# GRU state summed in place in PSUM, multiplied there, and copied to SBUF afterwards

## Chip, cores and metric

The kernel runs on one core of a Trainium2 chip. The metric is the device time of one execution in microseconds. Before the change, three runs gave 2057.22, 2060.13 and 2060.7 us; the median is 2060.13.

## What is computed

A recommendation model for 1024 users (the leading dimension of the inputs), each with 100 historical items of 128 features. A GRU runs over the items, an attention MLP scores every state against the target item, a softmax over time weights the states, and a second recurrence (AuGRU) uses the weighted sum. The part that the change touches is this:

```
def gru_step(h, x_t):
    gi = x_t @ gru_Wih.T + gru_bih
    gh = h @ gru_Whh.T + gru_bhh
    i_r, i_z, i_n = jnp.split(gi, 3, axis=-1)
    h_r, h_z, h_n = jnp.split(gh, 3, axis=-1)
    r = jax.nn.sigmoid(i_r + h_r)
    z = jax.nn.sigmoid(i_z + h_z)
    n = jnp.tanh(i_n + r * h_n)
    h_new = (1.0 - z) * n + z * h
    return (h_new, h_new)
...
feat = jnp.concatenate([keys, q, keys - q, q * keys], axis=-1)
score = _mlp(feat, [(att_W0, att_b0), (att_W1, att_b1), (att_W2, att_b2)], jax.nn.relu)
```

`keys` are the GRU states of all steps and `q` is the target item, so the first attention layer needs two data-dependent inputs for each step: the state h and the product q * h.

## The kernel before

Everything is held transposed: 128 features on the partitions, users along the free dimension. The 1024 users are two halves of 512, each an object of class Half. [...] All instructions are issued in an order written out by hand, and each engine works through its own list in that order; waits between engines are put in for each dependence on a tile or a buffer.

The GRU phase loops over the steps s from 0 to 99. In a step each half runs `gru` (L497): TensorE makes the gates pr, ph, pi and pz, each in a PSUM tile named ps, of which six buffers are used in turn (L222). Each gate is cut into four column groups of 32 that run beside each other. ScalarE makes r from pr (L520). VectorE makes u from ph and r (L528), adds it to pi in place (L538), ScalarE takes tanh of pi in place (L539) and the sigmoid of pz in place (L540), and VectorE ends with h - n, times z, plus n (L543, L544, L545). The last of these writes the new state hn to SBUF, where TensorE reads it as an operand in the next step. Between them VectorE transposes the state of the step before for storage (L557).

After the gates of both halves, `attend(s-1)` (L661) issues the attention matmuls for the state of the step before: hn with wk, the product kq with wkq, and the deeper layers (mv with w12) of earlier steps, all into two PSUM tiles pm (one for each half, two buffers, L223). `take(s-2)` (L694), run in the next step right after r of half 0, adds q0 to pm (f, L704) and applies the relu (mv, L709), and sends a row of scores to s_b. Directly behind `take`, `product(s-1)` (L579) multiplies the state of each half by the item, SBUF with SBUF (kq, L583). Scores of a block of steps are turned into softmax weights in three stages on VectorE (L750 to L799), one stage at a time, after half 0's gates. The stage called scores uses one of the two pm buffers for a transposed tile pt, which L760 reads.

GpSimd multiplies the inputs by the mask and sums them (L493, L494), and sums the weighted states (kw, L606, and pooled, L607). Its share of the pooling at the very end is done beside VectorE. Then come indirect gathers and the AuGRU phase, which is untouched by the change.

The SP queue issues nearly all loads and stores, in program order. At the start it loads wih, x of step 0 for half 0, the biases, x of step 0 for half 1, whh; then, from step 0's gates, x of steps 1 and 2 for both halves; then, in `attention_weights` (L225), item (512 KB) and the attention weights.

Of the kernel before, what the change touches and what calls it, by code (L numbers as in the profile page):

```python
# [9 lines left out]
F32 = mybir.dt.float32  # L10
# [9 lines left out]
P = 128  # L20
B = 1024
T = 100
HB = 512
NH = B // HB
# [13 lines left out]
QA, QB = (2, 3), (3, 2)  # L38
# [40 lines left out]
def kernel(ctx: ExitStack, tc: tile.TileContext, a: dict, out: bass.AP):  # L79
# [26 lines left out]
    nc = tc.nc  # L106
# [22 lines left out]
    item = const.tile([P, B], F32, name="item")  # L129
# [56 lines left out]
    def gru_phase(pools):  # L186
# [7 lines left out]
        x_second = xp.tile([P, HB], F32, name="x")  # L194
        nc.sync.dma_start(out=x_second, in_=a["hist_x"][0][:, HB:])
        whh = load("whh", [P, 3, P])
        pre = pools.enter_context(tc.tile_pool(name="pre", bufs=1))

        brz = const.tile([P, 2], F32, name="brz")
# [15 lines left out]
            nc.gpsimd.memset(s_bs[j], 0.0)  # L215
        q0 = pre.tile([P, B], F32, name="q0")

        hp = pools.enter_context(tc.tile_pool(name="hp", bufs=6))
        wp = pools.enter_context(tc.tile_pool(name="wp", bufs=2))
        sp = pools.enter_context(tc.tile_pool(name="sp", bufs=2))  # L220
        kp = pools.enter_context(tc.tile_pool(name="kp", bufs=3 * NH))
# [1 line left out]
        pa = pools.enter_context(tc.tile_pool(name="pa", bufs=2, space=PSUM))  # L223

        def attention_weights():  # L225
            nc.sync.dma_start(out=item, in_=a["item"])
            w0 = load("w0", [P, 4, A0])
            for i in range(NH):
                for f, s in F0[i]:
                    nc.vector.tensor_add(wk[i][:, f], w0[:, 0, s], w0[:, 2, s])  # L230
                    nc.vector.tensor_copy(wkq[i][:, f], w0[:, 3, s])
                    nc.vector.tensor_sub(wq[i][:, f], w0[:, 1, s], w0[:, 2, s])
                    for f1, s1 in F1[i]:
                        nc.sync.dma_start(out=w12[i][f, f1], in_=a["w1"][s, s1])
                    nc.sync.dma_start(out=bm[i][f, :], in_=a["b0"][s, :])
                sc = slice(SC[i], SC[i] + 1)
                for f1, s1 in F1[i]:
                    nc.sync.dma_start(out=w12[i][f1, sc], in_=a["w2"][s1, :])
                    nc.sync.dma_start(out=bm[i][f1, :], in_=a["b1"][s1, :])
                nc.sync.dma_start(out=bm[i][sc, :], in_=a["b2"].partition_broadcast(1))  # L240
# [219 lines left out]
        class Half:  # L460
            def __init__(self, i):
                self.i = i
                self.cols = ts(i, HB)
                self.ks = ts(i, KH)
                self.h = {}
                self.mv = self.first = None
                self.todo = []
                self.x = {0: x_second if i else x_first}
                self.m = {}
                self.kt = {}  # L470
                self.s_bs = s_bs[i::NH]


            def load(self, t, again=False):
                if t or again:
                    x = xp.tile([P, HB], F32, name="x")
                    nc.sync.dma_start(out=x, in_=a["hist_x"][t][:, self.cols])
                    self.x[t] = x
# [16 lines left out]


            def gru(self, t, after_gate, after_sum):  # L497

                x = self.x[t]
                h = self.h[t - 1] if t else hist[:, self.cols]  # L500
                hn = hp.tile([P, HB], F32, tag="h", name="hn")
                self.h[t] = hn

                def gate(g, parts):
                    p = ps.tile([P, HB], F32, tag="g", name=f"ps{g}")
                    for j, (w, v) in enumerate(parts):
                        for q in range(P // R):
                            nc.tensor.matmul(  # L508
                                p[ts(q, R), :],
                                lhsT=w[:, g, ts(q, R)],  # L510
                                rhs=v,
                                start=(j == 0),
                                stop=(j == len(parts) - 1),
                            )
                    return p

                both = ((wih, x), (whh, h)) if t else ((wih, x),)
                pr = gate(0, both)
                r = wp.tile([P, HB], F32, tag="r", name="r")
                nc.scalar.activation(r, pr, AF.Sigmoid, bias=brz[:, 0:1])  # L520
                after_gate()
                if t:
                    ph = gate(2, ((whh, h),))
                pi = gate(2, ((wih, x),))
                pz = gate(1, both)
                u = wp.tile([P, HB], F32, tag="u", name="u")
                if t:
                    nc.vector.scalar_tensor_tensor(  # L528
                        out=u,
                        in0=ph,  # L530
                        scalar=bhh[:, 2:3],
                        in1=r,
                        op0=ALU.add,
                        op1=ALU.mult,
                    )
                else:
                    nc.vector.tensor_scalar_mul(u, r, bhh[:, 2:3])
                nc.vector.tensor_add(pi, pi, u)  # L538
                nc.scalar.activation(pi, pi, AF.Tanh, bias=bih[:, 2:3])  # L539
                nc.scalar.activation(pz, pz, AF.Sigmoid, bias=brz[:, 1:2])  # L540
                after_sum()
                d = wp.tile([P, HB], F32, tag="d", name="d")
                nc.vector.tensor_sub(d, h, pi)  # L543
                nc.vector.tensor_mul(d, pz, d)  # L544
                nc.vector.tensor_add(hn, pi, d)  # L545

            def transpose(self, t):

# [20 lines left out]
            def store(self, q):  # L569
# [4 lines left out]
                    ],  # L574
                    in_=self.kt[q].rearrange("p k n c -> p k (n c)"),
                )


            def product(self, t):  # L579

                h = self.h[t]
                kq = wp.tile([P, HB], F32, name="kq")
                nc.vector.tensor_mul(kq, h, item[:, self.cols])  # L583
                self.first = h, kq


            def pool(self, count, eng):
# [68 lines left out]
        halves = [Half(i) for i in range(NH)]  # L656
# [4 lines left out]
        def attend(t):  # L661

            p = left[t] = [pa.tile([P, HB], F32, tag="a", name="pm") for _ in halves]

            old = [half.mv if t else hist[:, half.cols] for half in halves]
            k_rows = slice(0 if t <= T else 2 * R, P)

            def pack(i, q, w, v, start, stop):
                s = ts(q, R)
                nc.tensor.matmul(p[i][s, :], lhsT=w[:, s], rhs=v, start=start, stop=stop)  # L670

            def first(i, q, j):
                if t < T:
                    w = (wk, wkq)[j][i]
                    pack(i, q, w, halves[i].first[j], j == 0 and q != QB[i], j == 1)

            def more(i, q):
                pack(i, q, w12[i][k_rows, :], old[i][k_rows, :], True, q == QA[i] or t >= T)

            for turn in range(2 * NH):  # L680
                i, j = divmod(turn, 2)
                for q in range(2):
                    first(i, q, j)
                if i == 0:
                    for q in range(2, P // R):
                        more((QA, QB)[j].index(q), q)
                else:
                    for q in range(2, P // R):
                        first(QB.index(q), q, j)
# [128 lines left out]
        def gather_early(n):  # L818
            for _ in range(n):
                next(more_early)  # L820
# [3 lines left out]
        for s in range(T):  # L824
            last = s == T - 1
            n, due = divmod(s - again, 4)
            n, i = divmod(n, NH)
            more_history = 0 <= n < late

            def loads():  # L830
                for half in halves:
                    for m in range(1, AHEAD + 1) if s == 0 else (AHEAD,):
                        if s + m < T:
                            half.load(s + m)
                            if s + m >= late:
                                half.load_mask(s + m)
                    if s == T - AHEAD:
                        half.load_features()
                if more_history and due == 0:
                    halves[i].load(n, again=True)  # L840
                    halves[i].load_mask(n)

            def after_gate():
                if s:
                    take(s - 2)
                    for half in halves:
                        half.product(s - 1)
                loads()

            staged = None  # L850
            for half in halves:
                half.gru(
                    s,
                    after_gate if half.i == 0 else nothing,
                    (lambda: half.transpose(s - 1)) if s else nothing,
                )
                if half.i == 0:
                    staged = bool(soft["stages"])
                    stage(0 if last else 1)
# [35 lines left out]
                next(features[f])  # L895

        gather_early(4)
        take(T - 2)
        for half in halves:
            half.product(T - 1)  # L900
        attend(T - 1)
        stage(2)
        weights = soft["e"][0]
# [45 lines left out]
        for half in reversed(halves):  # L949
            t = blocked(s_bs[NH * (soft["j"] % 2) + half.i])  # L950
# [402 lines left out]
```

## Time and profile before

| what | value |
|---|---|
| median of three runs | 2060.13 us |
| the profiled execution's own time | 2054.49 us |
| its span in the profile | 2052.7 us |
| PE busy | 1998.8 us (97%) |
| DVE busy | 1763.7 us (86%) |
| ACT busy | 824.5 us (40%) |
| POOL busy | 1313.0 us (64%) |
| GRU loop, end of its gates | about 1386 us from the span's start |

The page gives one execution. A group's row names line, engine and operation, output and inputs by the program's names, the shape and the count; then the busy time in microseconds and the mean of one in ns; then the idle time of the engine just before and what ended it. PE is TensorE, DVE is VectorE, ACT is ScalarE, POOL is GpSimd, SP is the queue that issues loads and stores. A row of the timeline gives the start in microseconds from the span's start, the time taken, the engine, line and operation, and in brackets the idle time ahead of it and its releaser. Busy shares are averages over two phases: in slices of the page PE is at 90% or more nearly everywhere but for the first slice and those between 1400 and 1480 us.

### The profile page before, as it was taken

The numbers are of one execution on the slowest core, as the hardware profiler recorded it, in microseconds if no ns is written. First come the engines' busy times: TensorE is split into PE (matmuls) and PEld (weight loads), VectorE is DVE, ScalarE is ACT, GpSimd is POOL, SyncE is SP. The second block draws the span as 40 slices with busy tenths as digits, with TensorE's granted clock in tenths as the row PEclk, the third lists the DMA queues.
The fourth block names the chain that finished last, engine by engine and source line by source line (L and its number), as shares of the span: only waits on it lengthen the run. The fifth ranks groups of instructions, "written<-read, shape, count | busy, mean of one in ns | idle before, by whom it ended". The sixth has DMA issues, their size and how long they took to land.

```text
span 2052.7 us, 41040 instructions
## 1 busy us (share of the span) xinstructions
PE 1998.8 (97%) x15452; PEld 1049.1 (51%) x15452; DVE 1763.7 (86%) x3066; ACT 824.5 (40%) x1508; POOL 1313.0 (64%) x1291
## 2 busy tenths in 40 slices
PE   8999999999999999999999999998699999999998
PEld 4655433333455544444443333334344556679997
DVE  6888999998999999989999899997377777888886
ACT  3334343333434343434343343343244444445554
POOL 0234939569797969695979787998543354443431
PEclk9999999999999999999999999999799999999999
DMA  4453233332334334333433232333432333333332
GB/s 121 97 115 105 89 105 113 96 93 78 104 113 114 108 109 124 113 99 110 135 105 100 85 99 77 102 105 103 117 101 88 94 110 98 94 102 85 93 72 37
DMA packets 241643, 205.65 MB, mean 100 GB/s; under 512 B 59270, under 2 KB 204394, under 8 KB 241434
## 3 DMA queue, kind: packets, MB, share of 16 engines
q1 hardware_dynamic: 227498, 170.43, 29.4%
q0 software_dynamic: 12352, 32.31, 5.7%
q8 instruction: 123, 2.02, 0.4%
q14 instruction: 86, 0.70, 0.1%
q10 hardware_dynamic: 1584, 0.20, 0.1%
HBM read 146.82 MB, written 54.40 MB: 98 GB/s over the span
## 4 chain that ended last, share of the span: by engine, by line
PE 83%; DVE 9%; issue 2%; DMA 2%; ACT 1%; POOL 1%; another core or an unknown queue 1%; SPq 0%; DVEq 0%; ACTq 0%; POOLq 0%
PE ps L508 42%; PE pm L670 14%; PE ph L1076 5%; PE pr L1076 4%; PE pu L1076 4%; PE pr L1072 4%; PE pu L1072 4%; PE ph L1072 4%; DVE kq L583 1%; DMA rows<-keys_d,idx_k 1%; DVE ps L538 1%; DVE d L544 1%; DVE d L543 1%; DVE u L528 1%; ACT ps L539 1%
## 5 line engine op out<-in xcount | busy, mean ns | idle before, releaser
L508 PE MATMUL ps<-x,wih 128*32 128x512 f32 x4800 | 778.3, 595 | 4.6 <-DMA x<-in_hist_x 4.0
L508 PE MATMUL ps<-hn,whh 128*32 128x512 f32 x4752 | 768.1, 592 | 0.0
L508 PEld LDWEIGHTS ps<-x,wih 128*32 128x32 f32 x4800 | 260.2, 110 | 291.0 <-issue 270.2
L508 PEld LDWEIGHTS ps<-hn,whh 128*32 128x32 f32 x4752 | 258.2, 110 | 280.1 <-issue 271.9
L539 ACT ACTIVATE ps<-ps,bih 128x512 f32<-128x512 f32 x200 | 132.4, 662 | 546.5 <-DVE ps L538 546.5
L493 POOL TENSOR_TENSOR xm<-x,m 128x512 f32<-128x512 f32 x200 | 248.1, 1240 | 121.7 <-DMA m<-mask_d 60.8
L494 POOL TENSOR_TENSOR hist<-hist,xm 128x512 f32<-128x512 f32 x200 | 269.7, 1349 | 15.7
L174 POOL DMA_INDIRECT rows<-keys_d,idx_k x220 | 213.9, 972 | 86.5 <-POOL rows L173 50.0
L607 POOL TENSOR_TENSOR pooled<-pooled,kw 128x512 f32<-128x512 f32 x191 | 257.6, 1349 | 15.0
L670 PE MATMUL pm<-hn,wk 128*32 128x512 f32 x1200 | 257.1, 592 | 4.0 <-DVE f L704 2.3
L606 POOL TENSOR_TENSOR kw<-kt,e 128x512 f32<-128x512 f32 x191 | 220.1, 1153 | 62.2 <-DVE e L779 62.1
L670 PE MATMUL pm<-kq,wkq 128*32 128x512 f32 x1200 | 257.2, 592 | 0.0
L520 ACT ACTIVATE r<-ps,brz 128x512 f32<-128x512 f32 x200 | 137.6, 688 | 285.6 <-PE ps L508 285.1
L670 PE MATMUL pm<-mv,w 128*32 128x512 f32 (+1 forms) x808 | 240.5, 592 | 8.2 <-DVE e L760 8.2
L583 DVE TENSOR_TENSOR kq<-hn,item 128x512 f32<-128x512 f32 x200 | 233.0, 1204 | 0.0
L1084 ACT ACTIVATE c<-ph,bh 128x96 f32<-128x96 f32 (+41 forms) x198 | 96.4, 487 | 292.6 <-PE ph L1076 248.3
L173 POOL COPY rows<-rest 128x1 f32<-128x1 f32 x188 | 35.3, 188 | 215.4 <-DVE rest L1113 211.7
L543 DVE TENSOR_TENSOR d<-hn,ps 128x512 f32<-128x512 f32 x198 | 136.1, 687 | 34.9 <-ACT ps L539 32.4
L1100 DVE TENSOR_TENSOR pu<-pu,c 128x96 f32<-128x96 f32 (+41 forms) x197 | 88.2, 448 | 86.0 <-ACT c L1084 77.4
L538 DVE TENSOR_TENSOR ps<-ps,u 128x512 f32<-128x512 f32 x200 | 140.0, 700 | 23.7 <-PE ps L508 3.1
L544 DVE TENSOR_TENSOR d<-ps,d 128x512 f32<-128x512 f32 x200 | 138.3, 691 | 22.7 <-ACT ps L540 3.4
L704 DVE TENSOR_TENSOR f<-pm,q 128x512 f32<-128x512 f32 x200 | 128.0, 681 | 26.5 <-PE pm L670 26.4
(180 smaller groups left out, 3101.5 us busy)
## 6 DMA issues: line engine op xcount, KB each, us to landing
x<-in_hist_x SPq DMA_DIRECT2D x212, 256.0 KB
keys_d<-kt SPq DMA_DIRECT2D x48, 1024.0 KB
m<-mask_d SPq DMA_DIRECT2D x200, 128.0 KB
rows<-keys_d,idx_k POOLq DMA_INDIRECT x220
s_b<-mv SPq DMA_DIRECT2D x200, 8.0 KB
keys_d<-kt SPq DMA_DIRECT2D x32, 64.0 KB
at<-att_d SPq DMA_DIRECT2D x34, 48.0 KB
mask_i<-in_mask SPq DMA_DIRECT2D x8, 200.0 KB
```

What stands on the lines that cost most here:

```text
L174: nc.gpsimd.indirect_dma_start(out=r[:, at, :], out_offset=None, in_=keys_d[q], in_offset=bass.IndirectOffsetOnAxis(ap=idx_k[:, k, i : i + ...
L493: nc.gpsimd.tensor_mul(d, x, m)
L494: nc.gpsimd.tensor_add(acc, acc, d)
L508: nc.tensor.matmul(p[ts(q, R), :], lhsT=w[:, g, ts(q, R)], rhs=v, start=(j == 0), stop=(j == len(parts) - 1),)
L538: nc.vector.tensor_add(pi, pi, u)
L544: nc.vector.tensor_mul(d, pz, d)
L583: nc.vector.tensor_mul(kq, h, item[:, self.cols])
L606: eng.tensor_mul(d, k, w)
L607: eng.tensor_add(acc, acc, d)
L670: nc.tensor.matmul(p[i][s, :], lhsT=w[:, s], rhs=v, start=start, stop=stop)
L1072: nc.tensor.matmul(p, lhsT=m[:, 1, :], rhs=k, start=True, stop=False)
L1076: nc.tensor.matmul(p, lhsT=m[:, 0, :], rhs=v, start=False, stop=True)
```

## The change

The last sum of the GRU step writes the new state over n in the PSUM tile pi, and the product with the item is taken at once from there, as the next VectorE instruction. The copy of the state to the SBUF tile hn becomes a ScalarE instruction of its own (`keep`): for half 0 it is issued after r of half 1 in the same step, for half 1 after r of half 0 in the next step, ahead of `take`, and after the last step ahead of the final `take`. The method `product` and its calls go. The item is loaded by SP right after whh, since the product of step 0 now needs it within that step. The pool of hn has five buffers in place of six, that of kq four in place of two.

```
         whh = load("whh", [P, 3, P])
+        nc.sync.dma_start(out=item, in_=a["item"])
...
-        hp = pools.enter_context(tc.tile_pool(name="hp", bufs=6))
+        hp = pools.enter_context(tc.tile_pool(name="hp", bufs=5))
...
         def attention_weights():
-            nc.sync.dma_start(out=item, in_=a["item"])
             w0 = load("w0", [P, 4, A0])
...
-                self.mv = self.first = None
+                self.mv = self.copy = None
+                self.first = {}
...
                 nc.vector.tensor_sub(d, h, pi)
                 nc.vector.tensor_mul(d, pz, d)
-                nc.vector.tensor_add(hn, pi, d)
+                nc.vector.tensor_add(pi, pi, d)
+                kq = wp.tile([P, HB], F32, name="kq", bufs=2 * NH)
+                nc.vector.tensor_mul(kq, pi, item[:, self.cols])
+                self.first[t] = hn, kq
+                self.copy = hn, pi
+
+            def keep(self):
+
+                if self.copy is not None:
+                    nc.scalar.copy(*self.copy)
+                    self.copy = None
...
-            def product(self, t):
-
-                h = self.h[t]
-                kq = wp.tile([P, HB], F32, name="kq")
-                nc.vector.tensor_mul(kq, h, item[:, self.cols])
-                self.first = h, kq
...
-                    pack(i, q, w, halves[i].first[j], j == 0 and q != QB[i], j == 1)
+                    pack(i, q, w, halves[i].first[t][j], j == 0 and q != QB[i], j == 1)
...
             def after_gate():
+                halves[1].keep()
                 if s:
                     take(s - 2)
-                    for half in halves:
-                        half.product(s - 1)
                 loads()
...
-                    after_gate if half.i == 0 else nothing,
+                    after_gate if half.i == 0 else halves[0].keep,
...
         gather_early(4)
+        halves[1].keep()
         take(T - 2)
-        for half in halves:
-            half.product(T - 1)
         attend(T - 1)
```

## The prediction

> **What bounds the kernel now.** I read the page first: engines, slices, groups; then who waited for whom on TensorE, then the timeline of one step and of the end of the GRU phase. From the page, first the chain, then the DVE groups that the change touches and two like the new product:
>
> ```profile
> PE 83%; DVE 9%; issue 2%; DMA 2%; ACT 1%; POOL 1%; another core or an unknown queue 1%; SPq 0%; DVEq 0%; ACTq 0%; POOLq 0%
> L583 DVE TENSOR_TENSOR kq<-hn,item 128x512 f32<-128x512 f32 x200 | 233.0, 1204 | 0.0
> L543 DVE TENSOR_TENSOR d<-hn,ps 128x512 f32<-128x512 f32 x198 | 136.1, 687 | 34.9 <-ACT ps L539 32.4
> L538 DVE TENSOR_TENSOR ps<-ps,u 128x512 f32<-128x512 f32 x200 | 140.0, 700 | 23.7 <-PE ps L508 3.1
> ```
>
> TensorE carries 83% of the chain. The product at L583 takes 1204 ns where equal-sized operations with an operand in PSUM take 690 to 700. TensorE's waits inside the GRU loop (60 to 1398 us) are few:
>
> ```profile
> engine line waited for: us in total, times, longest us
> PE pm L670 <- DVE e L760: 8.2, 7, 2.1
> PE pm L670 <- DVE f L704: 2.3, 1, 2.3
> PE ps L508 <- DVE u L528: 0.7, 2, 0.5
> PE count L323 <- issue: 0.3, 1, 0.3
> ```
>
> So 1338 us of loop hold 11.2 us in which TensorE waits for VectorE, and no GRU change can take more out of it, since no matmul is removed. Asked in stretches of 20 us, the view puts these waits at about 240 to 265, 380, 500, 1300, 1340 to 1375 (2.5 us) and 1393: where softmax or sorting work is added to a VectorE that is already full. One ordinary step, from the timeline:
>
> ```profile
> 711.67 0.69 DVE L545 TENSOR_TENSOR hn<-ps,d 128x512 f32<-128x512 f32 x1
> 712.28 1.28 DVE L704 TENSOR_TENSOR f<-pm,q 128x512 f32<-128x512 f32 x2
> 713.45 0.69 ACT L520 ACTIVATE r<-ps,brz 128x512 f32<-128x512 f32 x1 [2.75 <-PE ps L508]
> 713.48 2.99 DVE L583 TENSOR_TENSOR kq<-hn,item 128x512 f32<-128x512 f32 x2
> 715.88 1.52 POOL L606 TENSOR_TENSOR kw<-kt,e 128x512 f32<-128x512 f32 x1
> 716.39 0.74 DVE L528 SCALAR_TENSOR_TENSOR u<-ps,bhh,r 128x512 f32<-128x512 f32 x1
> ```
>
> A step lasts 13.73 us (the r at L520 of half 0 began at 699.71 and again at 713.45). VectorE needs some 13.1 of it: two chains from u to hn of 4.46 us each (703.37 to 707.83), two sums f 1.2, two products 2.9. It keeps 0.6 us, less than any softmax stage. GpSimd's kw beside the products takes 1.52 us, elsewhere 1.07.
>
> **The Trainium skill.** "SBUF — State Buffer", Who interferes with whom: a VectorE instruction with two SBUF inputs contends with a GpSimd instruction that reads SBUF; one with at most one does not. The trace agrees: the first two products, with GpSimd idle, took 1.28 us together, later pairs up to 2.99. "PSUM — Partial Sum Buffer", PSUM bank collisions raise a hardware error: two engines may not touch one bank at once, two reads included. In the changed program's order the ScalarE copy indeed waits for the product, not only for the sum; no run here shows a collision.
>
> **The change part by part.** *Product.* 200 products go from 1204 ns to about 690 (L543, the same operand kinds): 200 x 0.51 = 103 us of VectorE, about 1.0 a step on average and 1.5 in steps such as that shown (2.9 to 1.4). Nearly all lies beside TensorE. Its worth is the stalls it ends. The product also leaves its place ahead of half 0's u and stands behind each hn sum: half 0's chain starts some 2.9 us sooner, half 1's u stands 0.69 later behind it, but not later than before.
>
> *Sum into PSUM.* 700 ns (L538) for 691 (L545): 200 x 0.01 = 2 us of VectorE, hidden.
>
> *Copy.* 200 ScalarE copies PSUM to SBUF. The nearest row is the copy at L1027, 128x512 out of PSUM in 0.58 us: 116 us more for an engine busy 40%. The state is usable 0.69 + 0.58 + about 0.1 = 1.4 us later than now. Half 0: its sum ends at 707.9, first use in the next step at 712.25; 4.3 us of cover. Half 1: its copy is queued behind the next step's r of half 0, which ends at 714.14, so the copy ends at about 714.8. TensorE's half-1 gates begin 12 weight-load groups of 0.43 us after the step's first load at 710.96: loads at 716.1, matmuls at 716.5, and they also need that copy, because pr of half 1 takes the PSUM buffer of pi of half 1 (six buffers in turn, eight tiles a step). Cover 1.7 us; with it gone, each missing 0.1 us costs 10 us over 100 steps. Behind the copy on ScalarE stand the two mv (0.6 each) and tanh; mv is used at the end of the step, 7 us later, and tanh waits for VectorE anyway. The s_b transfers behind mv on SP start 0.6 us later, needed steps later.
>
> *Buffers.* hn from 6 to 5: a buffer is rewritten after its last reader, the attention pack one step on. kq from 2 to 4: the same. Cost nothing.
>
> *Item load moved* ahead of four x loads on SP's queue: 512 KB. The DMA rates of the first 8 us add up to some 1.5 MB, and item ends 1.44 MB into the order, so it lands before the first product at 11.5. The x of step 1 comes 1.6 us later, about 9, needed at 11.4. Nothing lost. But the first steps have no slack: copy of half 0 ends at 12.9 where the state was used at 12.24; the sum of half 1 then ends at 16.3 (15.5 now), its product at 17.0, its copy at 17.7, and half 1's pr waits for that where it began at 16.5. VectorE begins step 1 some 0.2 later, and the product of half 0 stands ahead of half 1's u in the chain to the q0 activations that free the attention banks (25.85 now). Together about +0.9 us; bounds 0 and 2.5.
>
> *Gain in the loop.* With 1.0 to 1.5 us freed per step, VectorE has about 2 us free, and the scores of a stage end about 0.9 us before TensorE's attention pack instead of after it. In the last steps a stage costs some 2.3 us a step and just fits. I take all 8.9 us of the waits before 1380.
>
> *Gain at the end.* Now:
>
> ```profile
> 1391.66 0.69 DVE L545 TENSOR_TENSOR hn<-ps,d 128x512 f32<-128x512 f32 x1
> 1393.46 2.30 DVE L583 TENSOR_TENSOR kq<-hn,item 128x512 f32<-128x512 f32 x2
> 1395.68 0.71 DVE L756 STREAM_TRANSPOSE last<-s_b 128x512 f32<-128x512 f32 x1
> 1400.41 1.08 POOL L596 TENSOR_TENSOR pooled<-pooled,e 128x512 f32<-128x512 f32 x1 [0.61 <-issue]
> 1401.68 1.07 POOL L606 TENSOR_TENSOR kw<-kt,e 128x512 f32<-128x512 f32 x1 [0.20 <-DVE e L779]
> ```
>
> The last gates end at 1386.3 and the second f at 1399.7, and VectorE is busy throughout. Without its lag the last sum ends 2.4 us after the gates (0.3 to the gate's end, 0.65 sigmoid, 0.7 times z, 0.7 sum) instead of 6.0. One product behind it makes 3.1, the two f that free the attention banks 4.4, and the attention pack on TensorE 3.4 more: the next f starts 7.8 us after the gates, since the softmax stage (2.8 us on VectorE) is done by 7.2. Now it starts at 1398.5, 12.2 after the gates: a gain of 4.4. VectorE and TensorE thus arrive 8.9 - 0.9 + 4.4 = 12.4 us earlier. GpSimd does not: from 1329.7 it runs to 1400 without a real wait. It reaches 1329.7 earlier by the waits until then, 8.9 - 2.5 - 0.9 = 5.5, plus 1.3 for a wait on e that goes; from there it gains three contended pairs of kw and pooled (0.45 + 0.33 each), 2.3, and 0.4 of small waits. That is 9.5, and the later one counts: **-9.5 us**. From there to the AuGRU loop the chain passes through GpSimd's sums, gathers and transfers of unchanged length, and that loop is unchanged.
>
> 2052.7 - 9.5 = 2043.2 of span. The profiled execution took 2054.49 us, so 2045.0; the median of the runs is 5.6 above it, and the prediction is 2060.1 - 9.5 = 2050.6.
>
> **Rivals.** (a) *GpSimd does not hold the end*: what it stores up earlier is larger. For it: kw waits for e 12 times in the loop, 61.9 us. Against: 18 to 19 of each 20 us busy after 1280. -12.4 and 1 to 2 us more from rows no longer disturbed after 1400: 2046. (b) *Gain hidden*: VectorE's stages stay late because their small SBUF operations still meet GpSimd (L784, 32 columns, 1298 ns), and the start costs its full 2.5: half of 8.9 and of 4.4 stays, 6.6 is gained less 2.5, and GpSimd passes on about 3: 2057. (c) *Slower*: half 1's copy comes too late for the PSUM buffer. Place: pr of half 1, each step. It decides once the copy ends over 1.7 us later than I put it; half a microsecond beyond costs 50 us: 2110. Against: product and sum end near 713.0, before r. (d) *The product is no faster from PSUM*: nothing to gain but the order, 2059. Against: three groups at 690 to 700 ns with that operand.
>
> **How the numbers follow.** Likeliest 0.57, (a) 0.13, (b) 0.17, (c) 0.08, (d) 0.05. About 0.2% (4 us) is what a measurement of this kernel can tell from no change. Faster: 0.57 + 0.13 + half of (b) = 0.79; same: half of (b) and most of (d) = 0.12; slower 0.09. The likeliest alone spans 2046 to 2055 (start 0 to 2.5, gain at the end 2.2 to 6); with (a) and most of (b) the range is 2044 to 2058.
>
> **What would show it.** Right: the product near 690 ns, copies near 0.58 us, TensorE's waits on e and f under 2 us in the loop, kw near 1.08 everywhere, q0 about 1 us later at the start, the step still 13.73 us. Wrong: TensorE waiting for ScalarE at L508 step after step; products above 1 us; waits on e still several microseconds; a gain in the loop that does not reach the AuGRU phase.

## The result

Six runs of the changed kernel have a median of 2049.09 us (2044.58 to 2050.1); six runs of the kernel before beside them have 2059.01 us (2055.69 to 2060.7). The ratio is 0.9949, with a 95% interval of 0.9936 to 0.9962: about 10 us faster. The profiled execution took 2046.78 us with a span of 2045.0 us (before 2054.49 and 2052.7).

Of the page after, first the chain of work that ended last, then the groups of the GRU step (busy us, mean ns of one, then the idle time ahead of them and what ended it):

```profile
PE 92%; DVE 3%; DMA 2%; issue 1%; ACT 1%; another core or an unknown queue 1%; POOL 0%; SPq 0%; DVEq 0%; ACTq 0%; POOLq 0%
```

```profile
L539 DVE TENSOR_TENSOR ps<-ps,u 128x512 f32<-128x512 f32 x200 | 140.0, 700 | 21.5 <-PE ps L509 0.5 <-DVE u L529 0.5
L548 DVE TENSOR_TENSOR kq<-ps,item 128x512 f32<-128x512 f32 x200 | 138.2, 691 | 6.9
L544 DVE TENSOR_TENSOR d<-hn,ps 128x512 f32<-128x512 f32 x198 | 136.1, 687 | 35.6 <-ACT ps L540 35.2 <-issue 0.2
```

```profile
L555 ACT COPY hn<-ps 128x512 f32<-128x512 f32 x200 | 116.6, 583 | 92.3 <-DVE kq L548 92.3
L609 POOL TENSOR_TENSOR kw<-kt,e 128x512 f32<-128x512 f32 x191 | 206.0, 1078 | 70.6 <-DVE e L782 70.6
```

The product takes 691 ns instead of 1204, like its neighbours with a PSUM operand, which have not moved. The copy costs 583 ns, and what it waits for is the product (kq), not the sum. GpSimd's kw is at 1078 ns. VectorE's part of the chain fell from 9% to 3%. TensorE's waits in the GRU loop and its end (60 to 1398 us), by whom it waited for:

```profile
engine line waited for: us in total, times, longest us
PE pm L673 <- ACT hn L555: 2.5, 1, 2.5
PE pm L673 <- ACT mv L712: 0.4, 1, 0.4
```

All waits for e and f are gone; the one of 2.5 us stands after the last gates. One ordinary step, from the timeline (start, duration, idle time ahead in brackets):

```profile
703.30 0.70 DVE L546 TENSOR_TENSOR ps<-ps,d 128x512 f32<-128x512 f32 x1
704.03 0.69 DVE L548 TENSOR_TENSOR kq<-ps,item 128x512 f32<-128x512 f32 x1
704.95 1.08 POOL L609 TENSOR_TENSOR kw<-kt,e 128x512 f32<-128x512 f32 x1
705.27 1.29 DVE L707 TENSOR_TENSOR f<-pm,q 128x512 f32<-128x512 f32 x2 [0.55 <-PE pm L673]
706.99 0.69 ACT L521 ACTIVATE r<-ps,brz 128x512 f32<-128x512 f32 x1 [4.49 <-PE ps L509]
707.57 0.58 ACT L555 COPY hn<-ps 128x512 f32<-128x512 f32 x1
707.91 0.75 DVE L529 SCALAR_TENSOR_TENSOR u<-ps,bhh,r 128x512 f32<-128x512 f32 x1 [1.36 <-PE ps L509]
```

VectorE now waits for TensorE in an ordinary step (0.55 ahead of f, 1.36 ahead of u); before, its longest gap in such a step was 0.18 us. The copy of half 1 ends at 708.15. TensorE's matmuls of x for half 1 begin at 710.03, and those of hn, which read the copy, at 710.88. The wait for the copy stands at the last of four weight loads ahead of them:

```profile
710.46 0.25 PEld L509 LDWEIGHTS ps<-hn,whh 128*32 128x32 f32 x4 [0.18 <-issue]
```

That one begins at 710.60 in the trace, 2.45 us after the copy's end. This distance is called the copy's cover below. The end of the GRU phase, VectorE and GpSimd, then TensorE's last attention pack:

```profile
1380.37 0.69 DVE L548 TENSOR_TENSOR kq<-ps,item 128x512 f32<-128x512 f32 x1
1380.98 1.28 DVE L707 TENSOR_TENSOR f<-pm,q 128x512 f32<-128x512 f32 x2
1388.44 1.29 DVE L707 TENSOR_TENSOR f<-pm,q 128x512 f32<-128x512 f32 x2 [3.32 <-PE last L640]
1391.16 1.07 POOL L609 TENSOR_TENSOR kw<-kt,e 128x512 f32<-128x512 f32 x1 [2.71 <-DVE e L782]
...
1381.80 1.05 PE L673 MATMUL pm<-hn,wk 128*32 128x512 f32 x4 [2.55 <-ACT hn L555]
1385.15 1.44 PE L673 MATMUL pm<-kq,wkq 128*32 128x512 f32 x5
```

The gates end at 1374.83 (the first attention matmul behind them), 11.4 us sooner than before (1386.27). GpSimd waits 2.71 us for e: it does not hold the end. The last f starts 1.85 us after the pack ends at 1386.59.

To say where the time went I cut each trace at three points: the ninth r (loop entry, step 4 of half 0), the end of the last gates, and the first AuGRU state. The last column is the last f, from the gates' end.

| | loop entry | loop, to the gates' end | gates' end to first AuGRU state | last f |
|---|---|---|---|---|
| before | 59.28 | 1326.99 | 54.67 | 12.3 |
| changed | 60.68 | 1314.15 | 55.59 | 13.6 |
| difference | +1.40 | -12.84 | +0.92 | +1.3 |

That is -10.5 us up to the AuGRU phase. In this pair of traces 2.8 us of it are lost later, in code that did not change; in these two and the four traces of the first chip below (chips differ, see the experiments), its length from the second state on varies between 590.0 and 597.1 us, so the medians (-9.9) are the better measure of the whole.

### The profile page after: what moved, and what is told of

Read it like the earlier page. It is cut to its first block, busy times and chain, and to the rows that moved or that the text cites. A ratio compares the mean times of both kernels' runs of the same rounds, so it can differ in the third digit from the quotient of the medians.

```text
span 2045.0 us, 41241 instructions
## 1 busy us (share of the span) xinstructions
PE 1994.6 (98%) x15452; PEld 1176.7 (58%) x15452; DVE 1682.1 (82%) x3066; ACT 944.1 (46%) x1708; POOL 1260.7 (62%) x1291
## 4 chain that ended last, share of the span: by engine, by line
PE 92%; DVE 3%; DMA 2%; issue 1%; ACT 1%; another core or an unknown queue 1%; POOL 0%; SPq 0%; DVEq 0%; ACTq 0%; POOLq 0%
PE ps L509 48%; PE pm L673 16%; PE ph L1077 5%; PE pr L1077 5%; PE pu L1077 4%; PE pu L1073 4%; PE ph L1073 4%; PE pr L1073 4%; DMA rows<-keys_d,idx_k 1%; DVE ps L539 0%; DVE u L529 0%; DVE ps L546 0%; DVE d L545 0%; DVE d L544 0%
## 5 line engine op out<-in xcount | busy, mean ns | idle before, releaser
L509 PE MATMUL ps<-x,wih 128*32 128x512 f32 x4800 | 657.2, 594 | 4.4 <-DMA x<-in_hist_x 4.4
L509 PE MATMUL ps<-hn,whh 128*32 128x512 f32 x4752 | 650.1, 592 | 0.6 <-ACT hn L555 0.6
L509 PEld LDWEIGHTS ps<-x,wih 128*32 128x32 f32 x4800 | 281.7, 110 | 241.7 <-issue 220.4
L509 PEld LDWEIGHTS ps<-hn,whh 128*32 128x32 f32 x4752 | 279.6, 110 | 234.2 <-issue 212.0
L609 POOL TENSOR_TENSOR kw<-kt,e 128x512 f32<-128x512 f32 x191 | 206.0, 1078 | 70.6 <-DVE e L782 70.6
L673 PE MATMUL pm<-hn,wk 128*32 128x512 f32 x1200 | 237.7, 592 | 5.0 <-ACT hn L555 2.5
L673 PE MATMUL pm<-kq,wkq 128*32 128x512 f32 x1200 | 237.5, 592 | 0.0
L529 DVE SCALAR_TENSOR_TENSOR u<-ps,bhh,r 128x512 f32<-128x512 f32 x198 | 147.5, 745 | 73.1 <-PE ps L509 69.0
L673 PE MATMUL pm<-mv,w 128*32 128x512 f32 (+1 forms) x808 | 197.6, 592 | 0.5 <-ACT mv L712 0.4
L555 ACT COPY hn<-ps 128x512 f32<-128x512 f32 x200 | 116.6, 583 | 92.3 <-DVE kq L548 92.3
```

Of the source, the lines that this page charges most:

```text
L509: nc.tensor.matmul(p[ts(q, R), :], lhsT=w[:, g, ts(q, R)], rhs=v, start=(j == 0), stop=(j == len(parts) - 1),)
L529: nc.vector.scalar_tensor_tensor(out=u, in0=ph, scalar=bhh[:, 2:3], in1=r, op0=ALU.add, op1=ALU.mult,)
L609: eng.tensor_mul(d, k, w)
```

## The experiments

The theory is that the loop gained because VectorE's products no longer meet GpSimd, and that what limits the change is the cover of the copy, the start and the end. The first rival is that the gain is the order: product and chain sit in better places, wherever the product reads from. All times by stage come from the traces by the three cuts above. The kernels ran on three chips, on which the kernel before took 2056.1, 2031.2 and 2031.3 us (median); each ratio is to the kernel before on the same chip. Lines of the form A:B are stretches of a trace: start and end, length, then busy us and number of instructions of PE, PEld, DVE, ACT and POOL, then the granted clock (the share of its full clock that TensorE was allowed), the DMA share and GB/s.

**Order alone** (first chip). The product stands right behind the sum, but both use SBUF and there is no copy. Against the changed kernel:

```
-                nc.vector.tensor_add(pi, pi, d)
+                nc.vector.tensor_add(hn, pi, d)
...
-                nc.vector.tensor_mul(kq, pi, item[:, self.cols])
+                nc.vector.tensor_mul(kq, hn, item[:, self.cols])
...
-                self.copy = hn, pi
```

> The new order alone: the product stands right behind each sum as in the changed kernel, but the sum goes to SBUF as before and the product reads SBUF twice; no copy on ScalarE. Theory (what pays is the product's length, because VectorE is full): products stay near 1200 ns, TensorE's waits for VectorE in the loop stay, and the time is 2055 to 2060, at most 4 us under the kernel before. Rival (what pays is that the products no longer stand ahead of half 0's chain): the waits go all the same, and the time is 2047 to 2051, with products still above 1100 ns.

Measured: 2052.56 us, ratio 0.9981 (0.9972 to 0.9989), a time between the two bands and 3.5 us under the kernel before on this chip. Its loop took 1320.31 us, 6.7 less than before. But 3.4 us of it ran at half the clock, which happened in no other loop here:

```profile
1338.80:1342.10 3.30, 3.30 (x20) 1.02 (x16) 2.88 (x6) 1.24 (x2) 3.14 (x4) 0.50 1.07 325
```

A matmul took 1.06 us there instead of 0.59, so some 1.7 us were lost (estimated as half of the stretch). Without them the order gains about 8.4 of the 12.84. Its product's group, then TensorE's waits from 60 us to the phase's end:

```profile
L548 DVE TENSOR_TENSOR kq<-hn,item 128x512 f32<-128x512 f32 x200 | 174.9, 874 | 6.8
```

```profile
PE pm L672 <- DVE e L762: 4.2, 3, 2.1
PE pm L672 <- DVE f L706: 4.1, 1, 4.1
```

Neither theory had the 874 ns. I sorted the 200 products of each trace by how much of their length GpSimd's tensor operations lie beside them, at least half (beside) or under a twentieth (alone); the few in between are left out (number of products in brackets):

| | alone | beside GpSimd |
|---|---|---|
| before (SBUF) | 0.68 us (49) | 1.43 us (139) |
| order alone (SBUF) | 0.69 us (45) | 0.93 us (147) |
| changed (PSUM) | 0.69 us (51) | 0.69 us (144) |

The new order does not keep the products away from GpSimd, but each meeting costs less; why is open. So the order is worth about two thirds of the loop's gain, and a part of that again can be contention avoided; the waits for e halve but stay. The remaining 4.4 us or so come with the PSUM operand, which takes the same time alone and beside GpSimd.

**GpSimd made quiet, kernel before** (first chip). The masked sum and all of GpSimd's pooling but the first position are left out; VectorE's product stays where it was, from SBUF:

```
-                nc.gpsimd.tensor_mul(d, x, m)
-                nc.gpsimd.tensor_add(acc, acc, d)
...
-                    else:
+                    elif eng is nc.vector:
```

> The kernel before, in which GpSimd leaves out the masked sum of the inputs and its share of the pooling in every step; VectorE's instructions and their order are untouched. Theory (the product is long because two SBUF inputs contend with GpSimd): products near 650 to 700 ns, TensorE's waits for VectorE between 60 and 1380 us under 1.5 us, the last gates end 11 to 13 us earlier than in the kernel before. Rival (the product is long for another reason, its place or SBUF operands as such): products stay above 1000 ns and the waits stay.

Measured: 2038.61 us, ratio 0.9916 (0.99 to 0.9933). The loop took 1316.89 us, 10.1 less than before, with nothing moved. The gates end 10.1 us earlier, just short of the 11 to 13 expected, and the product stays just above its 700 ns. The product and TensorE's waits:

```profile
L580 DVE TENSOR_TENSOR kq<-hn,item 128x512 f32<-128x512 f32 x200 | 139.0, 735 | 0.0
```

```profile
PE pm L667 <- DVE f L701: 0.8, 1, 0.8
```

The shortfall has a place. In this execution the step from 950.6 lasted 16.9 us instead of 13.73, because TensorE worked slowly for some 6 us of it, at full clock and with nearly no listed wait (an undisturbed stretch first):

```profile
944.00:950.00 6.00, 6.00 (x61) 3.26 (x57) 5.48 (x12) 2.35 (x4) 0.00 (x0) 1.00 0.98 287
961.00:967.00 6.00, 5.32 (x26) 1.12 (x26) 1.94 (x3) 0.40 (x1) 2.69 (x3) 1.00 0.74 245
```

Its cause is open; no other loop here has it. Without these 3.2 us the loop would be 13.3 us shorter than before, as short as in the next experiment.

The unchanged product falls from 1204 to 735 ns by taking GpSimd's work away, and all but 0.8 us of TensorE's waits for VectorE go. The contention with GpSimd's work is thus the cause of most of what TensorE waited for. The experiment also frees VectorE's other SBUF operations from it, so it does not say that the product alone was to blame. Its total is no measure of the change, since GpSimd's work after the loop is shorter too (48.76 us from the gates' end to the first AuGRU state).

**GpSimd made quiet, changed kernel** (third chip). The same work left out of the changed kernel.

> The changed kernel without GpSimd's masked sum and with GpSimd's pooling for the first position only: the same work left out as in the quiet run of the kernel before, so its output is not the reference's. Theory (what the change gains in the loop is the contention with GpSimd, and it gains all of it): nothing is left to gain in the loop, where 95 steps of 13.73 us are 1304.4 us and the changed kernel takes 1306.6; last r of half 0 within 2.5 us of the changed kernel's; ratio to the kernel before as in the quiet run of the kernel before, 0.9906 to 0.9926. Rival (the new place of product and chain has a worth of its own at the end of the loop): the last sum and the last f come 2 us or more sooner after the gates than in the quiet run of the kernel before, and the ratio falls below 0.990.

Measured: 2011.58 us, ratio 0.9904 (0.9888 to 0.9921). The loop took 1313.70 us, only 0.45 less than the changed kernel's 1314.15: there the change had already won nearly all that there is. The ratio lies 0.0002 below the theory's band, well inside the interval. The rival's 2 us at the end are not there: the last sum ends 3.2 us and the last f starts 9.6 us after the gates, against 3.5 and 10.2 in the quiet kernel before. But both are some 2 us sooner than in the changed kernel with GpSimd at work (5.5 and, in the second profile below, 11.9), and TensorE's one wait shrinks:

```profile
PE pm L670 <- ACT hn L552: 1.0, 1, 1.0
```

So GpSimd still costs time at one place, the last steps, where VectorE's softmax stages (SBUF operations) run beside it.

**The changed kernel again** (third chip). No edit.

> The changed kernel once more, to see how much of its first profile repeats. Theory: the loop repeats to within 0.5 us (r of half 0 from the fifth step to the last: 1306.6 us), since it is bound by TensorE with no wait; the 1.85 us between the last attention pack and the last f does not come back (f 0.1 us after the pack), and the last f stands about 11.8 us after the gates instead of 13.6. Rival: the pause belongs to the kernel and comes back. Ratio 0.9936 to 0.9962 in either case.

Measured: 2018.95 us, ratio 0.9939 (0.9923 to 0.9956). The loop took 1314.12 us (1314.15 in the first profile), and the pause is gone; the last pack and the f behind it:

```profile
1384.79 1.44 PE L673 MATMUL pm<-kq,wkq 128*32 128x512 f32 x5
...
1386.34 1.29 DVE L707 TENSOR_TENSOR f<-pm,q 128x512 f32<-128x512 f32 x2 [1.58 <-PE pm L673]
```

The f starts 0.11 us after the pack, 11.9 us after the gates. The 1.85 us in the first profile are one execution's, not the kernel's (more on them under The end); without them the end is 0.4 us shorter than before instead of 1.3 longer.

**The copy of half 1 later.** Extra copies put it later by about 0.6 us each: one (third chip), two and four (first chip). The edit, here for two:

```
-                    nc.scalar.copy(*self.copy)
+                    for _ in range(3 if self.i else 1):
+                        nc.scalar.copy(*self.copy)
```

Two more:

> The changed kernel with the copy of half 1's state made three times in place of once, so that it ends about 1.2 us later. The cover was put at 1.7 us and is 1.9 in the changed kernel's trace: theory expects no stall and 2046 to 2053. Rival (the copy already limits TensorE, or ScalarE is short of time): 1.2 us in each of 100 steps, some 2160.

Four more:

> The same copy made five times, ending about 2.4 us later, 0.5 us beyond the cover. Theory: TensorE stalls about 0.5 us a step at the first matmul of half 1's gates, 2090 to 2120. Rival (the PSUM buffer of pi is not what TensorE waits for, only the use of the state one gate part, 0.86 us, later): 2047 to 2060.

And one more, expected after the results of these two:

> The copy of half 1 is made twice instead of once, 0.58 us later. Theory: the smallest cover of this copy is about 1.1 us, in the steps that follow an exponential, so 0.6 us more ends no matmul's cover: TensorE waits for the copy under 1 us in the loop, the last r of half 0 within 1 us of the changed kernel's, ratio within 0.001 of the changed kernel's on this chip (two such extra copies cost 10 us). Rival: every added copy costs in proportion, by other work queued behind it on ScalarE: half of the 10 us, ratio 0.002 to 0.003 above the changed kernel's.

| extra copies | delay | loop | median, ratio to before |
|---|---|---|---|
| none | 0 | 1314.15 | 2049.09, 0.9949 |
| one | 0.6 us | 1314.99 | 2018.33, 0.9936 (0.9919 to 0.9952), third chip |
| two | 1.2 us | 1326.28 | 2055.97, 1.0003 (0.9994 to 1.0012) |
| four | 2.5 us | 1382.69 | 2114.25, 1.0279 (1.0262 to 1.0296) |

TensorE's waits for the copy inside the gates, with two and then with four more:

```profile
PE ps L509 <- ACT hn L556: 7.6, 15, 1.5
```

```profile
PE ps L509 <- ACT hn L556: 38.9, 26, 2.6
```

Two more were expected to cost little, by a cover of 1.9 us that was read at the matmuls of x; the time lies above the band, and the loop lost 12 us. Ordinary steps lost nothing: 1.2 of their 2.45 us are left. The loss lies in the steps that follow an exponential. One of these in the changed kernel, TensorE's matmuls of x for half 0 and its weight load ahead of hn among ScalarE's instructions:

```profile
292.55 1.28 ACT L779 ACT_TABLE_LOAD   x1
293.85 0.44 ACT L779 ACTIVATE e<-e 128x288 f32<-128x288 f32 x1
294.31 1.28 ACT L521 ACT_TABLE_LOAD   x1
295.45 2.02 PE L509 MATMUL ps<-x,wih 128*32 128x512 f32 x16
295.60 0.69 ACT L521 ACTIVATE r<-ps,brz 128x512 f32<-128x512 f32 x1
296.19 0.58 ACT L555 COPY hn<-ps 128x512 f32<-128x512 f32 x1
298.46 0.25 PEld L509 LDWEIGHTS ps<-hn,whh 128*32 128x32 f32 x4 [0.18 <-issue]
```

The same place with two more copies:

```profile
295.00 2.02 PE L509 MATMUL ps<-x,wih 128*32 128x512 f32 x16
295.78 0.69 ACT L521 ACTIVATE r<-ps,brz 128x512 f32<-128x512 f32 x1
296.36 1.81 ACT L556 COPY hn<-ps 128x512 f32<-128x512 f32 x3
298.23 0.47 PEld L509 LDWEIGHTS ps<-hn,whh 128*32 128x32 f32 x8 [0.39 <-ACT hn L556]
```

Two table loads of 1.28 us and the exponential hold r of half 0, and the copy queued behind it. In the changed kernel the copy is ready at 296.77 and the load that waits for it stands at 298.60, a cover of 1.8 us. Two extra copies take 1.2 of it, and in their run ScalarE is also 0.6 us further behind: r begins 0.78 us after the matmuls of x, in the changed kernel 0.15. Together that is the whole cover.

It can be less still. In four softmax blocks of the changed kernel a VectorE operation on SBUF operands (L773, otherwise at most 0.43 us, and never more with GpSimd quiet) took 1.35 to 1.52 us, and the exponential, r and the copy came late with it. In the two steps behind each of these the cover is 0.05 to 0.9 us (0.6 and 0.9 also in steps 95 and 96). One of them, with the copy's end at 1177.41 and the load that waits for it at 1177.53:

```profile
1168.87 1.51 DVE L773 TENSOR_TENSOR e<-e,top 128x256 f32<-128x256 f32 x1
1176.83 0.58 ACT L555 COPY hn<-ps 128x512 f32<-128x512 f32 x1
1177.47 0.17 PEld L509 LDWEIGHTS ps<-hn,whh 128*32 128x32 f32 x4 [0.26 <-issue]
```

One extra copy therefore does not quite stay inside the cover. It costs 0.8 us in the loop, in steps 37, 38, 91, 92 and 98; the bounds expected for it hold, with no such wait of a matmul in the list and the ratio unchanged, but not the smallest cover of 1.1 us that they were drawn from.

With four more, an ordinary step is at the edge and not over it; one such step:

```profile
705.35 0.69 ACT L521 ACTIVATE r<-ps,brz 128x512 f32<-128x512 f32 x1 [2.80 <-PE ps L509]
705.94 3.04 ACT L556 COPY hn<-ps 128x512 f32<-128x512 f32 x5
708.54 1.04 PE L509 MATMUL ps<-x,wih 128*32 128x512 f32 x8
709.04 0.13 PEld L509 LDWEIGHTS ps<-hn,whh 128*32 128x32 f32 x4 [0.37 <-ACT hn L556]
719.09 0.69 ACT L521 ACTIVATE r<-ps,brz 128x512 f32<-128x512 f32 x1 [2.80 <-PE ps L509]
```

The copies end at 708.98. The matmuls of x for half 1 begin before that, at 708.54: they do not wait for pi's PSUM buffer. The load ahead of hn comes 0.07 us later than its usual gap of 0.30, and the step lasts 13.74 us. Of the loop's steps 45 keep 13.73 us, and the other 50, around the softmax stages, lose the 68 us, up to 3.6 us in one. So the expected time came, 2114 in 2090 to 2120, but not by the stall expected, half a us in every step. On the place the rival was right: TensorE waits for the use of the state. The rival's time (2047 to 2060) missed all the same.

**The start.** Step 0 as before: its sums go to SBUF, its products are taken in step 1 (second chip).

```
+                if t == 0:
+                    nc.vector.tensor_add(hn, pi, d)
+                    return
...
+                if s == 1:
+                    for half in halves:
+                        half.product(0, half.h[0])
```

> The changed kernel, but step 0 as before: its state goes straight to SBUF, its products are taken in step 1 from SBUF, and there is no copy for it. The changed kernel enters its steady loop 1.4 us later than the kernel before. Theory (the start is longer because copy and product stand in a chain without slack): the loop is entered about 1.0 us earlier than in the changed kernel, and 0.5 to 1.5 us of the time go. Rival (the start is longer because of the item load): no change at the start.

Measured: 2018.87 us, ratio 0.9938 (0.9924 to 0.9951). Loop entry came at 61.44 us, but TensorE's first attention pack ran at half the clock:

```profile
27.60:31.00 3.40, 3.40 (x20) 1.91 (x16) 0.46 (x1) 0.00 (x0) 0.00 (x0) 0.50 0.69 196
```

That cost some 1.6 us. With the same start in the combined run below, at full clock, entry came at 59.88, for 60.22 in the end run below, which has the changed start. At most some 0.3 us are to be had, not 1. TensorE's wait for q0 did not shrink (3.0 to 3.2 us, for 2.5), and so this expectation missed.

**The item load where it was relative to x** (second chip): behind the four loads of x.

> The changed kernel with the item loaded behind the four x loads of steps 1 and 2, as in the kernel before, but still ahead of the attention weights. Theory: the x loads are in time either way and the item is needed at about 11.9 us, so the start is unchanged within 0.5 us. Rival (the earlier item load delays the inputs): TensorE enters the loop 0.5 to 1.5 us earlier.

Measured: 2018.85 us, ratio 0.9943 (0.993 to 0.9957); loop entry 61.16, 0.9 later than in the end run below. Both expectations missed: the item now comes too late for the first product, the only group of products with a DMA ahead of it:

```profile
L547 DVE TENSOR_TENSOR kq<-ps,item 128x512 f32<-128x512 f32 x200 | 138.2, 691 | 7.7 <-DMA item<-in_item 0.9
```

The move of the load is thus worth 0.9 us at the start; the total does not show it.

**The end.** The 1.85 us ahead of the last f could have been due to the small feature matmuls that TensorE runs before it; this kernel issues them behind that `take` (second chip):

```
+        take(T - 1)
         some(0, 1)
-        take(T - 1)
         some(0, 1)
```

> The changed kernel with the final feature matmuls some(0, 1) issued behind take(T - 1) in place of ahead of it. In the changed kernel the f behind the last attention pack begins 1.85 us after the pack's last matmul, and the trace names those feature matmuls. Theory (f waits for them): f begins within 0.3 us of the pack's end, GpSimd's kw and the start of the AuGRU phase come 1.5 to 2 us earlier. Rival (f waits for something else): it begins as late as before, and the time stays.

Measured: 2017.87 us, ratio 0.9941 (0.9927 to 0.9954); f starts 0.11 us after the pack. But the item run and the unedited second profile, with the end unchanged, show the same, so the theory falls. What the first profile's trace does show is that f waits for a semaphore update of the pack's last matmul: the matmul ends at 1386.59, the update is recorded at 1388.35, together with those of three later matmuls (to 1388.49); in the second profile it comes 0.02 us after the matmul's end. Why it was late is open.

**Start and end together** (second chip), the two edits in one kernel:

> Both edits, step 0 as before and the feature matmuls behind take(T - 1). The sum of what each gives: 1.5 to 3.5 us under the changed kernel if both theories hold, 2045.5 to 2048; no difference if neither.

Measured: 2018.63 us, ratio 0.9941 (0.9927 to 0.9954). It does not differ from the changed kernel within the intervals, and no kernel here that does the whole work is faster than it by more than the intervals.

What was not tried is the product from PSUM in its old place: pi's buffer would then have to live into the next step.

## Why the prediction was right, and where it was not

The forecast was -9.5 us, to 2050.6; measured was -9.9, to 2049.09. The total is right; its terms are so only in part. The -9.5 was GpSimd's own sum, and GpSimd did not hold the end; for VectorE and TensorE -12.4 was said, and of that the loop brought 3.9 us more and the end about 4 less. That these errors nearly cancel is luck.

*The product and the copy.* 690 ns was said and 691 measured; 0.58 and 0.583; the sum stays at 699, kw falls to 1078. For the cause the prediction used the Trainium skill, "SBUF — State Buffer", Who interferes with whom: two SBUF inputs on VectorE contend with a GpSimd instruction that reads SBUF, one does not. The quiet run bears it out with 735 ns for an untouched SBUF product, and the table with 0.69 us for the PSUM product beside GpSimd. The order by which the copy waits for the product was read from "PSUM — Partial Sum Buffer", PSUM bank collisions raise a hardware error: two engines must not be at one bank at once, two reads included. The copy's row shows the wait; no run here shows a collision.

*Gain in the loop: said 8.9, measured 12.8.* The step took TensorE's waits for VectorE as the ceiling ("no GRU change can take more out of it"). That was wrong: the waits that the view lists are not all of the time lost. After the change the view lists none in the loop, and the loop is 12.8 us shorter. The trace of the kernel before shows where the rest was. Nine steps carry the 8.9 us of listed waits, and each is longer than 13.73 us by its wait and 0.2 to 0.35 us more, one (from 1331.2) by 1.1 more; two others (from 223.3 and 532.2) are 0.24 and 0.68 longer with no wait listed. TensorE's matmuls last 0.59 us and follow each other every 0.43, in four column groups beside each other, so a short delay of one need not leave a gap in the records; that this is the reason is argued, not shown. The right ceiling would have been the length itself: from the ninth r to the last of half 0 there are 95 steps, which took 1319.4 us and at 13.73 would take 1304.4. Of the 15 us between, 1.2 belong to one step that is longer in the changed kernel too.

*Start: said +0.9, measured +1.40 in the first pair.* In the bounds (0 to 2.5). 0.4 of it is that TensorE waited 4.4 us for x in that execution, for 4.0 before; in four later traces with the same start and a wait of 4.0 to 4.1 the entry stands at 60.22 to 60.34, about 1.0 later than before. So the size was right. The mechanism, copy and products in the chain to q0, was confirmed for a small part: taking them out of step 0 gave at most 0.3 us back, and the rest is open.

*Gain at the end: said 4.4 for VectorE, measured 0.4 at most.* The step had the last sum 2.4 us after the gates; it ends 5.5 after them (before 6.1). It assumed that VectorE no longer lags at that point. It still does: the softmax stage of the step before holds the last step's half-0 chain, and TensorE waits 2.5 us for the copy. With GpSimd quiet it is 3.2, so most of the rest of the lag goes with GpSimd's work beside that stage, which the change does not remove. The last f came 13.6 us after the gates where 7.8 was said; 1.85 of it is the pause that did not come back.

*GpSimd holds the end at -9.5: wrong.* It waited for e 1.3, 1.1 and 2.7 us in the last steps (0.95 at the last one in the second profile, without the pause), so the rival that GpSimd does not hold the end was right on this. That rival's time (2046) did not come since its gain at the end did not. The sum that holds is 1.4 - 12.8 + 0.9 = -10.5 up to the AuGRU phase.

*The copy's cover: said 1.7, measured 2.45 in ordinary steps, 1.8 behind most exponentials and under 1 in ten steps.* The step had the place wrong: it let pr of half 1 wait for pi's PSUM buffer, and TensorE waits one gate part later, for the state. It also looked at one ordinary step only. The slower rival is a real edge, but not where it put it: 0.6 us more delay costs 0.8 us, 1.2 us makes the change worth nothing, and 2.5 us gives 2114 us. That this is close to the 2110 it named, for half a us in each step, is luck: the ordinary steps lost nothing.

## What to carry to other kernels

Where VectorE is full and shares SBUF with a busy GpSimd, an operand taken from PSUM (or the same operation at another moment) can be worth far more than its instruction count, and a copy on a less loaded engine is a fair price. Measure the gain to be had by the length of the stage against its undisturbed steps, not by the sum of the listed waits. Before queueing a copy behind another engine's work, find its cover in the worst step (here behind a ScalarE table switch, and worst where a VectorE stage ahead of it met GpSimd), not in a typical one. Before reading a stretch's length as the edit's, look at the granted clock in it.

## What was not expected of the hardware

- The same SBUF product took 1204, 874 or 735 ns on average, by its place in the order or the absence of GpSimd's work. Beside GpSimd it took 1.43 us before and 0.93 in the new order, alone 0.68; with an operand in PSUM 0.69 in either case.
- Single executions held stretches that are not their edit's: 3.4 us at half the granted clock in the loop of the order run and at the first attention pack of the start run, 3.2 us lost at full clock in one step of the quiet run, and a semaphore update 1.8 us late in the first profile.
- The chips differ by some 25 us for the same kernel. In the first pair and on the first chip, 15 to 21 us lie between the first and the second AuGRU state, while gathers are awaited; on the other two, 6. The phase behind that takes 580.8 to 581.3 us there, for 590.0 to 597.1. After the gates 20 to 38 us run at half clock in the former and 7 to 10 in the latter, of which at most half can be lost, so that accounts for a part at best; the rest is open. The ratio of the change agrees within its interval in both places where it was measured (0.9949 and 0.9939).
